# One attention kernel's opening: the first pair of heads projected from all of x and its tokens chosen by 0/1 products

## The chip, the core and the metric

The kernel runs on one core of a Trainium2 chip. A core has a matrix engine (PE, with its weight loads PEld), a vector engine (DVE, VectorE), a scalar engine (ACT, ScalarE), a general engine (POOL, GpSimd) and a sync engine (SP) that here only issues DMAs. Each engine runs its instructions in order; engines wait for each other by semaphores. The metric is the device time of one execution in microseconds (us); three executions give a median.

## The reference

x is (8, 512, 1024): batch, features, tokens; the mask is (8, 1024) of zeros and ones. Cut to what matters:

```python
xt = transpose(x, (0, 2, 1))
q = xt @ Wq.T                                   # queries = keys = values
qh = q.reshape(B, T, 8, 64).transpose(0, 2, 1, 3)
scores = einsum('bhqd,bhkd->bhqk', qh, qh) / 8
logits = (scores * cmask + (1 - cmask) * -1e30) * rmask
attn = softmax(logits)
out = (einsum('bhqk,bhkd->bhqd', attn, qh) -> (B, T, 512)) @ Wo.T
return x + transpose(out, (0, 2, 1))
```

Columns of masked tokens get no weight. Rows of masked tokens have all logits zero, so their context is the plain mean of all values.

## The kernel before, in words

Only kept tokens (mask 1) go through the attention. A batch's kept tokens are compacted into NK columns (NK = 544 here, LONG = 576 is the other size); the last column, NK - 1, carries the batch's mean token, which serves all masked ones. A path for the case that neither size suffices works on all tokens.

**Stages.** `early()` runs once, ahead of a branch; `late(n)` is the attention for n columns. Between them the count of kept tokens (`verdict`) is loaded into a register of every engine, and a branch picks `late(LONG)`, `late(SHORT)` or neither; in program order `late(LONG)` stands first and `late(SHORT)`, which runs here, behind it. At the end a flag is loaded, and a second branch guards the path for all tokens.

**Opening.** `early()` loads the mask and batch 0 of x (`load_batch`, L379: 8 pieces of 256 KB), builds an identity and small constants on POOL, turns the mask into columns (`mcol`), counts ranks of kept tokens by products with a triangle (`rank_t`, L1069 to L1070) and counts per batch (`kept_t`). Batch 0 is turned to rows of tokens by 32 PE transposes (`turn_first`, L406), copied by ACT (L412) and stored in DRAM (`xd`, L416). VectorE sums the rows of x for the mean (`mean_first`, L421) and finds, for each of the NK places, the token that belongs there (`search`, L488: it counts ranks not above the place, over 1024, 896, 768, 640 and 512 columns). Behind the branch, POOL loads Wq (L990), ACT puts its columns in order (`order_columns`, L999), POOL gathers the rows of the kept tokens (`gather`, L500: five indirect DMAs), PE turns them back (`collect`, L513) between the turning of Wq (`turn_weights`, L1009), and the first pair is projected (`project`, L544).

**Pairs.** The attention runs over 32 pairs of heads (8 batches, four pairs each; `pairs[p]`). A pair has five chunks of keys in the order LAST, 0, 1, 2, 3: the chunk LAST is the 64 columns from 512 on (`s` L648, `el` L651), the others have 128 (`s` L626, exponentials `e` L634 with their row sums). Between the chunks, `slots_of(p)` places other work: the contexts of the pair before (`attend_short`, `attend_half`, L672), the projection of the pair after next, its turned values (`turn_values`, `copy_values`), squared lengths and the bound for the softmax (`lengths_of` L592, `bias_of` L605 to L610), and, in the third pair of a batch, the mean and the collecting of the next batch (`put_mean`, `collect`). Dictionaries keyed by (pair, slot) place the turning of later batches by VectorE (`TURN`, L432, stored by SP in four DMAs per quarter, L440), the sums of features by ACT (`FEATURES`, L451), `SEARCH`, `GATHER`, the loads (`LOAD`) and the output's fetches. Names with `_LATER` hold for batch 0 alone. The whole order is written out by hand.

**Buffers.** x has two tiles of half a batch (`x`, bufs = NN = 2), so a batch is loaded into what the batch before leaves. PSUM has two score tiles of two banks (`s`) and four single banks (`t`).

Of the kernel before, what the change touches and what calls it, by code (L numbers as in the profile page):

```python
# [10 lines left out]
F32 = mybir.dt.float32  # L11
# [295 lines left out]
def attention_of_kept_tokens(ctx, tc, x, mask, wq, wo, out, ident, wqT, woT, verdict, flag):  # L307
# [52 lines left out]
    homes = [keep.tile([B * NT, P], F32, name=f"home_{i}") for i in range(2)]  # L360
    seen = {}
# [38 lines left out]

    def turn_first(i):

        r, at = divmod(i * P, NB)
        pt = bank(f"xt_0_{i}")
        for d in range(ND):
            nc.tensor.transpose(pt[:, d * P : (d + 1) * P], xs[0][r][:, d, at : at + P], ident)  # L406
        if i == 0:
            xds[0] = dr.tile([T + 1, D], F32, tag="xd_0", name="xd_0", bufs=1)
            nc.sync.dma_start(xds[0][T : T + 1, :], zero)
        tag = "oc" if i < NC else "xin"  # L410
        xt = sb.tile([P, D], F32, tag=tag, name=f"xt_0_{i}", bufs=NC)
        nc.scalar.copy(  # L412
            xt.rearrange("p (a d f) -> p a d f", a=A, d=ND),
            pt.rearrange("p (d a f) -> p a d f", d=ND, a=A),
        )
        nc.sync.dma_start(xds[0][i * P : (i + 1) * P, :], xt)  # L416

    def mean_first():
        xbars[0] = keep.tile([P, ND, NN], F32, name="xbar_0")
        for r in range(NN):  # L420
            nc.vector.tensor_reduce(xbars[0][:, :, r], xs[0][r], axis=AX.X, op=ALU.add)  # L421
# [43 lines left out]
    def place_ranks(b):  # L465
        rank = sb.tile([P, T], F32, tag="rank", name=f"rank_{b}", bufs=1)
        found = sb.tile([P, NC], F32, tag="found", name=f"found_{b}")
        if b:
            source = sb.tile([P, NC], I32, tag="source", name=f"source_{b}")
        else:  # L470
            source = keep.tile([P, NC], I32, name="source_0")
        searches[b] = rank, found, source
# [35 lines left out]
    def collect(b, i):  # L508
# [8 lines left out]
        nc.scalar.copy(  # L517
            xcs[b][:, :, i * P : i * P + m],
            pt[:, : ND * n].rearrange("p (d n) -> p d n", d=ND)[:, :, :m],
        )  # L520

# [79 lines left out]
    def bias_of(pair):  # L601
# [7 lines left out]
        biases[pair] = sb.tile([P, NC], F32, tag="bias", name=f"bias_{b}_{pr}")  # L609
# [325 lines left out]
    def slots_of(p):  # L935

        b, pr = pairs[p]
# [8 lines left out]
        if p == 0:  # L946
            todo[0].append(lambda: project(behind, 1))
            todo[1].append(lambda: values(behind))
        if behind:
            if p == 0:  # L950
                todo[2].append(lambda: lengths_of(behind))
            elif p != ND - 1:
                todo[1].insert(0, lambda: lengths_of(behind))
        late = p == 2
        if pr == 2 and b + 1 < B:
            at = (2, 2, 2, 3, 3) if late else (1, 2, 2, 2, 2)
            todo[at[0]].append(lambda: put_mean(b + 1))
            for i in range(NC):
                todo[at[i]].append(lambda i=i: collect(b + 1, i))
        if p == ND - 1:  # L960
            todo[3].append(lambda: values(behind))
            todo[3].append(lambda: lengths_of(behind))
        if ahead:
            for hf in range(2):
                todo[4 if late else 3].append(lambda hf=hf: project(ahead, hf))
        if ahead and not late:
# [27 lines left out]
    def order_columns(w, nm):  # L994

        ws = []
        for e in range(ND):
            t = sb.tile([P, D], F32, tag="g", name=f"{nm}_in_order_{e}", bufs=NT)
            nc.scalar.copy(  # L999
                t.rearrange("p (a d f) -> p a d f", a=A, d=ND),  # L1000
                w[e].rearrange("p (a f d) -> p a d f", a=A, d=ND),
            )
            ws.append(t)
        return ws

    def turn_weights(wT, nm, d):
# [5 lines left out]
        nc.scalar.copy(wT[:, d, :], pt)  # L1012

    def early():
# [3 lines left out]
        load_batch(0)  # L1018
# [27 lines left out]
        )  # L1046
        for ri in ris:
            nc.gpsimd.memset(ri, 1.0)

# [13 lines left out]
        nc.vector.tensor_copy(spread, totals.unsqueeze(2).to_broadcast([BC, 2, P]))  # L1063
        pt = bank("mcol_t")
        nc.tensor.transpose(pt[:, :BC], mrow, ident[:BC, :BC])
        mcol = keep.tile([P, BC], F32, name="mcol")
# [8 lines left out]
        nc.tensor.matmul(pk[:, B : B + 1], spread[:, 1, :], ones[:BC, 0:1], start=True, stop=True)  # L1075
        rank = keep.tile([BC, P], F32, name="rank_row")
# [3 lines left out]

        tc.mark_branch_hint_location("over", "LikelyTaken", engines=ENGINES)
        place_ranks(0)
        for r in range(NN):
            pt = bank(f"rank_{r}")
            for i in range(G):
                chunk = r * G + i
                nc.tensor.matmul(
                    pt[:, i * P : (i + 1) * P],
                    ident[:BC, chunk : chunk + 1].to_broadcast([BC, P]),
                    rank,  # L1090
                    start=True,
                    stop=True,
                )
            nc.scalar.copy(searches[0][0][:, r * NB : (r + 1) * NB], pt)  # L1094
            if r == 0:
                for i in range(NT):
                    turn_first(i)

        nc.vector.tensor_scalar(key[DK:P, LAST:NC], key[DK:P, LAST:NC], float(-DK), None, ALU.add)
# [6 lines left out]

        nc.vector.memset(low, 1.0)
        nc.vector.memset(lowest, 1.0)
        nc.vector.memset(flag, 1)
        for b in range(B):  # L1110
            nc.vector.tensor_scalar(pads[:, b, :], key, kept[:, b : b + 1], None, ALU.is_ge)
# [290 lines left out]
```

## Time and profile before

| what | value |
|---|---|
| median of 3 runs | 689.88 us (689.59 to 691.09) |
| the profiled execution's own time | 689.0 us |
| its span, first to last instruction | 687.3 us |
| PE busy | 645.6 us, 94% |
| ACT / DVE / POOL busy | 397.2 / 359.4 / 182.5 us |
| mean granted PE clock | 0.974 |
| DMA | 116.37 MB, 169 GB/s |
| first scores (s, L648) start | 40.06 us |
| second, third, fourth, fifth pair's first scores | 58.11, 72.97, 91.82, 108.71 us |

The busy time by slices of the span (40 slices of 17.2 us each; digits are tenths, 9 is 90% or more):

```profile
PE   6489999999999999999999999999999999999953
PEld 5456566656565655556565655555565656554422
DVE  5235676335464654747464654836564434724462
ACT  4566668755584657655584656665675556454400
POOL 3540310130044202450144202450144102334040
PEclk9799999999999999999999999999999999999985
```

PE is dense from the fourth slice on and thin in the first three; PEclk is the clock that PE was granted. The most costly groups of PE are the scores, contexts, projections and the output product:

```profile
L626 PE MATMUL s<-qT 64*128 64x272 f32 x1024 | 170.1, 417 | 2.9 <-ACT el L651 1.0
L672 PE MATMUL av<-e,v 128*64 128x272 f32 x1024 | 131.4, 399 | 0.0
L544 PE MATMUL pq<-xc,wqT 128*128 128x272 f32 x512 | 124.8, 397 | 0.0
L793 PE MATMUL po<-woT,cT 128*128 128x512 f32 (+1 forms) x448 | 107.5, 434 | 0.0
```

The columns of such a group: line, engine, operation, output from input, shapes, count, then busy us and the mean ns of one, then idle time just ahead and what ended it. A float32 product appears as two records, a transpose as one. Matmul ends are modelled, so the mean of one includes its latency; the pitch of a row of them is the time of the stretch by their number.

### The profile page before, as it was taken

How to read it: one execution, taken by the hardware profiler on the slowest of the kernel's cores; microseconds unless marked ns; L12 is line 12 of the kernel's file. 1: busy time of each engine (PE TensorE's matmuls, PEld its weight loads, DVE VectorE, ACT ScalarE, POOL GpSimd, SP SyncE). 2: the span in 40 equal slices, each digit the busy share in tenths (PEclk: the TensorE clock that was granted, in tenths of full speed). 3: DMA queues.
4: the chain of work that ended last, by engine and by line, in shares of the span. 5: the costliest groups of instructions: out<-in, count | busy, mean ns of one | idle time of the engine just before them, and what ended most of it. 6: DMA issues, size and time to landing. Idle time of an engine off the chain costs nothing.

```text
span 687.3 us, 12044 instructions
## 1 busy us (share of the span) xinstructions
PE 645.6 (94%) x4139; PEld 391.5 (57%) x4139; DVE 359.4 (52%) x1049; ACT 397.2 (58%) x1059; POOL 182.5 (27%) x306
## 2 busy tenths in 40 slices
PE   6489999999999999999999999999999999999953
PEld 5456566656565655556565655555565656554422
DVE  5235676335464654747464654836564434724462
ACT  4566668755584657655584656665675556454400
POOL 3540310130044202450144202450144102334040
PEclk9799999999999999999999999999999999999985
DMA  6473832451766568854876477865764473339358
GB/s 230 155 240 90 253 89 68 141 158 45 169 182 212 155 171 209 269 181 115 210 191 207 156 182 193 261 193 137 190 195 127 114 184 100 113 119 251 84 174 260
DMA packets 96969, 116.37 MB, mean 169 GB/s; under 512 B 10312, under 2 KB 74312, under 8 KB 96896
## 3 DMA queue, kind: packets, MB, share of 16 engines
q1 hardware_dynamic: 80144, 75.13, 40.4%
q0 software_dynamic: 12528, 38.25, 17.4%
q10 hardware_dynamic: 4224, 2.10, 1.0%
q8 instruction: 35, 0.57, 0.3%
q14 instruction: 38, 0.31, 0.1%
HBM read 72.78 MB, written 42.67 MB: 168 GB/s over the span
## 4 chain that ended last, share of the span: by engine, by line
PE 84%; DMA 6%; ACT 3%; DVE 2%; issue 2%; SPq 1%; POOL 1%; POOLq 0%; ACTq 0%; DVEq 0%
PE s L626 21%; PE av L672 19%; PE pq L544 16%; PE po L793 14%; PE s L648 3%; PE xc L513 3%; PE v L569 2%; PE pa L821 2%; PE top L605 1%; ACT e L634 1%; DMA xr<-in_x_dram 1%; DMA xd<-xt 1%; DMA row<-rt 1%; DMA g<-od,origin 1%; PE xt L406 1%
## 5 line engine op out<-in xcount | busy, mean ns | idle before, releaser
L634 ACT ACTIVATE e<-s,bias 128x544 f32<-128x544 f32 x256 | 180.4, 710 | 69.4 <-PE s L626 63.2
L626 PE MATMUL s<-qT 64*128 64x272 f32 x1024 | 170.1, 417 | 2.9 <-ACT el L651 1.0
L626 PEld LDWEIGHTS s<-qT 64*128 64x128 f32 x1024 | 97.7, 186 | 70.6 <-issue 28.9
L672 PE MATMUL av<-e,v 128*64 128x272 f32 x1024 | 131.4, 399 | 0.0
L544 PE MATMUL pq<-xc,wqT 128*128 128x272 f32 x512 | 124.8, 397 | 0.0
L544 PEld LDWEIGHTS pq<-xc,wqT 128*128 128x128 f32 x512 | 97.4, 195 | 18.6 <-issue 0.8
L793 PE MATMUL po<-woT,cT 128*128 128x512 f32 (+1 forms) x448 | 107.5, 434 | 0.0
L672 PEld LDWEIGHTS av<-e,v 128*64 128x64 f32 x1024 | 67.9, 136 | 56.0 <-issue 23.1
L805 POOL DMA_DIRECT2D od<-oc x56 | 30.2, 551 | 251.3 <-ACT oc L803 251.1
L793 PEld LDWEIGHTS po<-woT,cT 128*128 128x128 f32 (+1 forms) x448 | 46.9, 150 | 46.9 <-issue 46.1
L907 POOL DMA_INDIRECT g<-od,block_origin x56 | 57.0, 1017 | 27.1 <-issue 12.4
L867 DVE STREAM_TRANSPOSE o<-g 128x512 f32<-128x512 f32 x56 | 39.3, 702 | 42.6 <-DMA g<-od,block_origin 42.6
L651 ACT ACTIVATE el<-s,bias 128x544 f32<-128x544 f32 x32 | 22.8, 714 | 59.8 <-PE s L648 44.9
L663 DVE CUSTOM_DVE_ANT_0 junk<-el,part 128x272 f32<-128x272 f32 x64 | 28.3, 442 | 53.4 <-ACT el L651 41.2
L592 DVE TENSOR_REDUCE len<-sq 128x10 f32<-128x640 f32 x32 | 26.2, 818 | 52.3 <-ACT sq L590 52.3
L552 ACT COPY qT<-pq 128x272 f32<-128x272 f32 x64 | 24.4, 381 | 49.9 <-PE pq L544 48.3
L903 POOL COPY step<-e 1x1 f32<-1x1 f32 x77 | 15.9, 206 | 136.2 <-ACT e L634 105.7
L634 ACT ACTIVATION_READ_ACCUMULATOR e<-s,bias 128x1 f32 x256 | 50.3, 197 | 0.0
L500 POOL DMA_INDIRECT xin<-xd,source x40 | 39.5, 987 | 20.3 <-issue 6.9
L870 DVE TENSOR_TENSOR xr<-o,xr 128x512 f32<-128x512 f32 x56 | 38.8, 693 | 9.9 <-DMA xr<-in_x_dram 6.9
L607 DVE TENSOR_REDUCE m<-top 128x1 f32<-128x128 f32 x32 | 9.3, 291 | 63.4 <-PE top L605 63.4
L488 DVE TENSOR_SCALAR_CACHE_REDUCE junk<-rank,key 128x1024 f32<-128x1024 f32 (+4 forms) x40 | 40.0, 999 | 3.4 <-ACT rank L1094 2.4
(147 smaller groups left out, 671.0 us busy)
## 6 DMA issues: line engine op xcount, KB each, us to landing
x<-in_x_dram SPq DMA_DIRECT2D x56, 256.0 KB
xd<-xt SPq DMA_DIRECT2D x112, 128.0 KB
xr<-in_x_dram SPq DMA_DIRECT2D x28, 512.0 KB
out_dram<-xr SPq DMA_DIRECT2D x24, 512.0 KB
rb<-row SPq DMA_DIRECT2D x60, 160.0 KB
od<-oc POOLq DMA_DIRECT2D x28, 256.0 KB
rank<-ranks SPq DMA_DIRECT2D x6, 512.0 KB
xd<-xt SPq DMA_DIRECT2D x8, 256.0 KB
```

The costliest lines, as they stand in the source:

```text
L488: nc.vector.tensor_scalar(junk[:, :n], rank[:, i * P :], key[:, col], 0.0, ALU.is_le, ALU.add, accum_out=found[:, col])
L500: nc.gpsimd.indirect_dma_start(out=xin[:n, :], out_offset=None, in_=xds[b], in_offset=bass.IndirectOffsetOnAxis(ap=searches[b][2][:n, i : ...
L544: nc.tensor.matmul(pq[:, :KH], wqT[:, d, pr * P : (pr + 1) * P], xcs[b][:, d, cols], start=(d == 0), stop=(d == ND - 1),)
L626: nc.tensor.matmul(ss[h][:, hf, :KH], qT[heads[h], keys], qT[heads[h], queries[hf]], start=True, stop=True,)
L634: nc.scalar.activation(e[:, :, h, :], ss[h][:, :, :KH], AF.Exp, bias=bias, scale=SCALE, accum_out=sums[pair[1] % 2][:, h, c : c + 1],)
L663: nc.vector.tensor_tensor_reduce(junk[:, :KH], e[:, 0, h, :], parts[b], 1.0, 0.0, ALU.mult, ALU.add, ends[pr % 2][:, h : h + 1])
L672: nc.tensor.matmul(av[head, :KH], v[keys, c, head], e[keys, hf if c < LAST else 0, h, :], start=(c == first), stop=(c == last),)
L793: nc.tensor.matmul(po[k * n : (k + 1) * n, :w], cTs[b, pr][:, i * P : i * P + n], woT[:, pr, k * w : (k + 1) * w], start=(pr == 0), stop=( ...
L805: nc.gpsimd.dma_start(ods[b][places[i], k * w : (k + 1) * w], oc[k * n : (k + 1) * n, :w])
L867: nc.vector.transpose(o.rearrange("p k t -> p (k t)"), gs[b, i])
L870: nc.vector.tensor_tensor(to, o, to, ALU.add)
L907: nc.gpsimd.indirect_dma_start(out=g, out_offset=None, in_=ods[b], in_offset=bass.IndirectOffsetOnAxis(ap=block_origin[:, b, i : i + 1], a ...
```

## The change

Batch 0's first pair no longer waits for the compacted tokens. `early()` now loads the first rows of Wq (into woT's space) and x, and `project_first` projects **all** 1024 tokens onto the first pair's 128 features (`tall`), copies that (`q`), and multiplies it with 0/1 matrices (`chosen`, made by VectorE: `place == count`), which yields the compacted queries (`short`). The bound of that pair comes from the squared lengths of all tokens times the mask. Its tokens' places are found by ACT with Sign and a sum (`search_first`) and turned into sources by one operation. x is turned by VectorE (32x32 blocks, `turn_first`) in place of PE, and stored by SP and POOL. Idle transposes (`warm`) stand around the mask's transpose. Wq's turning, batch 0's mean, collecting and the projections for the second and third pair move into the first pair's slots, with VectorE making the copies. Batch 1's loads move from POOL to SP, and the tables for batch 0 shift. The branch keeps `late(SHORT)` directly behind `early()`; `late(LONG)` goes into the last branch, with an opening of its own.

```diff
+    def load_first():
+        xs[0] = [None] * NN
+        for r in reversed(range(NN)):
...
+                nc.sync.dma_start(
+                    xs[0][r][:, d, :],
+                    x[0].rearrange("(p d) t -> d p t", d=ND)[d][..., r * NB : (r + 1) * NB],
+                )
     def turn_first(i):
-        pt = bank(f"xt_0_{i}")
...
+        xt = sb.tile([P, n // Q, P], F32, tag="xt", name=f"xt_0_{i}", bufs=2)
+        nc.vector.transpose(
+            xt.rearrange("p k (d f) -> p k d f", d=ND),
+            xs[0][r][:, :, at : at + n].rearrange("p d (k t) -> p k d t", t=Q),
+        )
+        for a in range(A):
+            to = xds[0][i * n : (i + 1) * n, a * P : (a + 1) * P]
+            queue = nc.gpsimd if a % 2 else nc.sync
+            queue.dma_start(to.rearrange("(k t) c -> t k c", t=Q), xt[a * Q : (a + 1) * Q, :, :])
+    def add_first(r):
...
+        nc.vector.tensor_reduce(xbars[0][:, :, r], xs[0][r], axis=AX.X, op=ALU.add)
+    def warm(n):
+        pt = bank("warm")
+        for i in range(n):
+            nc.tensor.transpose(pt[:, :P], ident, ident)
+    def choose(i, S):
+        nc.vector.tensor_scalar(S, count[:, : S.shape[1]], place[:, i : i + 1], None, ALU.is_equal)
+    def search_first(rank):
...
+            nc.scalar.activation(
+                sign[:, i * P :], pr[:, i * P :], AF.Sign,
+                bias=half[:, i : i + 1], scale=-1.0, accum_out=found[:, i : i + 1],
+            )
+    def project_first(chosen, mcol):
+        wT = sb.tile([P, ND, P], F32, tag="junka", name="wqT_0", bufs=1)
+        pw = bank("wq_0_t")
+        for d in range(ND):
+            nc.tensor.transpose(pw[:, d * P : (d + 1) * P], woT[:, 0, d::ND], ident)
+        nc.scalar.copy(wT.rearrange("p d e -> p (d e)"), pw)
+        search_first(seen["rank"])
...
+        for i in reversed(range(NT)):
+            project_all(i)
+            if i % 2 == 0:
+                copy_two(i)
+            if i % G == 0:
+                square(i // G)
+        order_columns()
+        turn_first(2)
+        turn_first(3)
+        for i in (3, 2, 1, 0):
+            choose(i, chosen[i])
+        sources_of_first()
+        turn_first(0)
+        turn_first(1)
...
+        lengths(1)
+        lengths(0)
...
+        for i in reversed(range(NT)):
...
+                    nc.tensor.matmul(
+                        short[:, hf, :n],
+                        q[i // G][:, i % G, :],
+                        chosen[i][:, hf * H : hf * H + n],
+                        start=(i == NT - 1),
+                        stop=(i * P <= hf * H),
+                    )
+            if i == G:
+                tops[pairs[0]] = first_top
+                bias_of(pairs[0], first_bias)
+        add_first(1)
+        add_first(0)
+        mean_of(0)
+        nc.scalar.copy(
+            rings[0][:, :LONG].rearrange("p (h n) -> p h n", h=2), short[:, :, :H]
+        )
...
     def slots_of(p):
-        if p == 0:
-            todo[0].append(lambda: project(behind, 1))
-            todo[1].append(lambda: values(behind))
...
-            at = (2, 2, 2, 3, 3) if late else (1, 2, 2, 2, 2)
+            at = (3, 3, 4, 4, 4) if late else (1, 2, 2, 2, 2)
...
+        if p == 0:
+            for d in range(ND):
+                todo[d // 2].append(lambda d=d: turn_weights(wqT, "wq", d, nc.vector.tensor_copy))
+            todo[2].append(lambda: put_mean(0))
+            for i in range(NC):
+                todo[(2, 2, 3, 3, 3)[i]].append(lambda i=i: collect(0, i, nc.vector.tensor_copy))
+            for hf in range(2):
+                todo[3].append(lambda hf=hf: project(behind, hf))
+            todo[4].append(lambda: values(behind))
+            todo[4].append(lambda: lengths_of(behind))
+            for hf in range(2):
+                todo[4].append(lambda hf=hf: project(ahead, hf))
+            todo[4].append(project_first_mean)
+            todo[4].append(lambda: values(pair))
+            todo[4].append(lambda: bias_of(behind))
+        elif p == 1:
+            todo[0].insert(0, lambda: values(behind))
+        elif p == ND - 1:
+            for hf in range(2):
+                todo[1 + hf].append(lambda hf=hf: project(behind, hf))
...
     def late(n):
-        weights["wq"] = order_columns(load_weights(wq, "wq", nc.gpsimd), "wq")
+        queries_of(0)
+        load_batch(1)
...
         for i in range(NC):
             gather(0, i)
...
+        nc.vector.tensor_copy(
+            qT[:, NK:W].rearrange("p (r k) -> p r k", k=END),
+            qT[:, NK - END : NK].unsqueeze(1).to_broadcast([P, (W - NK) // END, END]),
+        )
...
-        TURN_LATER = [(0, 2), (0, 4), (1, 0), (1, 1)]
+        TURN_LATER = [(0, 4), (1, 0), (1, 1), (1, 2)]
+        FEATURES_LATER = {(1, 1): (0,), (1, 2): (1,), (1, 3): (2,), (1, 4): (3,), (2, 0): (4, 5), (2, 1): (6, 7)}
-        GATHER_LATER = {(1, 4): (0, 1, 2), (2, 0): (3,), (2, 1): (4,)}
+        GATHER_LATER = {(1, 4): (0,), (2, 0): (1,), (2, 1): (2,), (2, 2): (3,), (2, 3): (4,)}
...
-        with tc.If(fit > SHORT - 1, label="over") as over:
-            with tc.If(fit < LONG):
...
+    kept_tokens(SHORT)
+    again = nc.values_load(flag[0:1, 0:1], min_val=0, max_val=1)
+    with tc.If(again > 0, label="again"):
+        kept_tokens(LONG)
...
```

More of the change, by code (lines that the diff above doesn't have):

```diff
@@ L935, in slots_of @@
     def slots_of(p):
-        b, pr = pairs[p]
+        b, pr = pair = pairs[p]
         todo = [[] for _ in range(NC)]
@@ L1079, in early @@
         seen["mrow"], seen["rank"] = mrow, rank
[L1081 to L1099, printed above, removed]
+        nc.vector.tensor_tensor(place, pc[:, :NT], mcol[:, :NT], ALU.mult)
+        nc.vector.tensor_scalar(place, place, -1.0, None, ALU.add)
         nc.vector.tensor_copy(kept, pk[:, 0:B])
@@ L1109, in early @@
         nc.vector.memset(flag, 1)
-        for b in range(B):
-            nc.vector.tensor_scalar(pads[:, b, :], key, kept[:, b : b + 1], None, ALU.is_ge)
-        nc.vector.tensor_scalar(pens, pads, NEG, None, ALU.mult)
-        mean_first()
-        for i in range(NC):
-            search(0, i)
-        mean_of(0)
     def place_all():
@@ L1202, in late @@
                 scores(pair, c)
-                if k == (4 if p == ND - 1 else 3) and p + 1 < len(pairs):
+                if k == (4 if p == ND - 1 else 3) and 0 < p < len(pairs) - 1:
                     bias_of(pairs[p + 1])
```

232 lines of the change are left out of this document (160 added, 72 removed).

## The prediction

> **What bounds the kernel now.** I read the busy time by stretches first, then the chain of waits of the first 110 us, then the timeline of the opening, and last the opening in steps of 1 us for the clock. The stretches (columns: PE, PEld, DVE, ACT, POOL busy with counts, granted clock, DMA share, GB/s):
>
> ```profile
> 130.00:210.00 80.00, 79.73 (x527) 48.06 (x524) 39.57 (x121) 51.07 (x141) 19.78 (x33) 1.00 0.55 154
> ...
> 450.00:530.00 80.00, 79.56 (x552) 47.28 (x550) 44.08 (x125) 48.69 (x133) 24.00 (x39) 1.00 0.62 171
> ```
>
> From 130 us to 610 us PE is busy 79.6 of every 80 us. Nothing can be won there by overlap, and a shift of its start is a shift of the end. So the opening decides. The chain there:
>
> ```profile
> 14.98 7.01 DMA xd<-xt
> ...
> 22.90 3.43 DMA xin<-xd,source
> ...
> 40.13 0.62 PE s L648 x8
> ...
> 58.11 0.69 PE s L648 x8
> ...
> 108.71 0.62 PE s L648 x8
> ```
>
> The s L648 rows shown open the first pair of heads, the second, and the fifth, which is batch 1's first (batch 0 has four). Ahead of 40.13 batch 0 goes out to DRAM (7.01 us), comes back by row gather (3.43 us), is turned (PE xc L513 from 26.46), and is projected (pq L544 from 32.31). From the fifth pair on, both kernels issue the same instructions in the same order on each engine, so the change is worth what it moves 108.71. The timeline of the opening:
>
> ```profile
> 8.48 2.29 DVE L421 TENSOR_REDUCE xbar<-x 128x4 f32<-128x2048 f32 x1
> ...
> 11.33 2.29 DVE L421 TENSOR_REDUCE xbar<-x 128x4 f32<-128x2048 f32 x1 [0.56 <-DMA x<-in_x_dram]
> ...
> 21.75 0.17 DVE L458 TENSOR_TENSOR mean<-total,quadrant 128x16 f32<-128x16 f32 x1
> ...
> 25.65 0.17 DVE L1139 TENSOR_SCALAR lacks<-kept 128x8 f32<-128x8 f32 x1 [3.72 <-issue]
> ```
>
> x's row sums cost 4.58 us, hidden now under the turning of x. The branch on the number of kept tokens costs VectorE 3.72 us. The clock, by single microseconds:
>
> ```profile
> 29.00:30.00 1.00, 1.00 (x7) 1.00 (x6) 0.00 (x0) 0.61 (x2) 0.94 (x1) 0.50 0.51 193
> 30.00:31.00 1.00, 1.00 (x10) 1.00 (x9) 0.00 (x0) 0.85 (x2) 0.04 (x1) 0.92 0.04 12
> ...
> 51.00:52.00 1.00, 1.00 (x4) 0.77 (x3) 0.93 (x4) 0.97 (x4) 0.00 (x0) 0.50 0.00 0
> ...
> 54.00:55.00 1.00, 1.00 (x5) 0.80 (x5) 0.00 (x0) 0.39 (x1) 0.00 (x0) 0.97 0.92 170
> ```
>
> PE comes to full clock about 3.6 us after it turns dense (26.46 to 30.1, 50.4 to 54.0) and drops after some 4.7 us of idling (15.3 to 20). Four 128x128 transposes took 0.85 us at half clock, 0.44 at full. The records say 1.00 for the first 19 us, but there too the transposes took 0.85 a group until about 13 us: PE began at half clock.
>
> **The change, part 1: up to the first scores.** Removed from in front of them: the turning of x by PE (32 transposes), its round trip, the turning of Wq, the collecting, the first projection. Added, in PE's order:
>
> Seven and six idle transposes (about 0.21 us each at half clock) fill PE from 1.48, when the identity stands, around mcol_t; rank_t, kept_t and the new place_t (four short records, by kept_t about 0.8) run to about 7.2. The turn of Wq's first rows (0.85) ends at 8.0; those rows are one 256 KB piece put ahead of x, which moves x by about 1 us (1 MB took about 4): its last half, awaited at 11.33 in L421, to 12.3, its first, in use at 8.1, to 9 at the latest. Then 16 rank records (3.4, at half clock), to 11.5.
>
> The tall projection is 64 records of 128 columns: 13.7 us at half clock, 7.0 at full, by the transposes' pitch. The short products: 16 records of 288 columns before the bound (pq: 3.88 us for 16 of 272, so 4.1), then 2.3 us.
>
> If the clock comes up only in the tall products, after one dense stretch like those above, say at 16.4: 23 records are slow, tall ends at 20.9, the first short products at 25.0. If it comes up by 8 to 9, rank ends at 9.5, tall at 16.5 (x's last half is there in time), short at 20.6.
>
> Behind that everything is VectorE in order: the top's transpose and three small steps (1.1, from top L605 to bias L610), the two row sums, now behind the bound (4.6, by L421), mean and constants (0.5), the branch, lacks and the 96 end columns (0.4). The branch now falls through instead of jumping. No row shows that, so between 0 and 3.72; I take 2.0, the middle, for the jump is the only kin. First scores: 25.0 + 8.6 = 33.6 in the late case. In the early case VectorE itself is later than PE (last half of x turned, pads and lengths to about 22.1), and they come at 22.1 + 8.4 = 30.5. The rank products of 6 to 8 us did not raise the clock before 13, which speaks for late, the longer dense stretch for early: 32.5. This moves the opening by 40.1 - 32.5 = 7.6 us.
>
> [...]
>
> Beside this path: eight choosing operations (576 wide, 0.45 to 0.75 us each by 64x128 TENSOR_SCALAR, 0.22, and the 640 wide search, 0.87) and four STREAM_TRANSPOSE of 1.23 fit before 19 us, while PE is in the tall products; without that cover they cost up to 8. With two xt tiles the third turning waits until the first one's stores have landed, and behind it stand pads, lengths and the bound; VectorE waits for the sign counts until about 16.5 anyway, so some 3 us of it are covered. The five sign counts replace VectorE's searches: 3456 columns at ACT's 0.70 per 544, 4.5 us, under the tall products. order_columns (4.07) lies under the short ones. The stores of x are 16 issues instead of 8, half of them on POOL, ahead of its branch, the two part masks (2.0) and the gathers, which start near 24 and land near 32; PE asks for them 5.5 us after the first scores, so 6 us of cover. On SP, batch 1's loads come behind those stores and wait for the row sums to free x's tiles, 28 to 31; they are turned only at the end of the first pair.
>
> **Part 2: from the first scores to 108.71.** Before, 68.6 us. PE's work in it, by the chain's rows at full clock: scores 4 x 5.2, contexts 3 x 4.44, nine half projections of 1.94, values 5 x 0.55, collecting 2.2, Wo 1.74, bounds 1.1, together 59.4; 9.2 us are waits and slow clock, 5.7 of them in the first pair (18.0 us long, with 12.4 of PE work). The change puts into that pair what it took out of the opening: Wq's 16 transposes 1.74, collecting 2.2, half a projection 1.94, values 0.55, the mean's column 0.15, so 6.6 more: 66.0. Of the 9.2 us that were lost, some go, for the first pair now holds 18.4 us of PE work. What remains: PE idles about 5 us before the first scores and starts them slow (1.7), score buffers wait for ACT (about 1.2), copies between projections and values (0.6), and 4 us in the other three pairs, as before, with one new wait: the last gather of batch 1 is asked for one chunk before its transposes, where it had two to three, about 1.3 us. I take 7.5: 73.5. VectorE's nine copies out of PSUM (0.69 each by the 128x512 sum of L845, no less than the 0.44 of the 272 wide L710) lie under the pair's 18 us.
>
> Sum: 32.5 + 73.5 = 106.0 against 108.71: 2.7 us sooner. Against the profiled span of 687.3, 684.6; with the 1.7 around it 686.3. That execution (689.0) lay 0.9 below the median of the three runs, so 687.2.
>
> [...]
>
> **The rivals.**
> - Early: clock full by 9 us, branch nearly free. For it: 7 us of dense PE before the tall products. Against: 6 to 13 us before. First scores at 30.5 or, with the branch at 0.5, near its lower bound, 29: 2 to 3.5 more, 683.7 to 685.2.
> - A wash: the opening's 7.6 us come back as deferred work. For it: 6.6 us of it are PE's, and PE is the bound; with the waits as large as before (9.2 us) the part is 75.2, first scores at 33.5 then end at 108.7: 690.
> - Slower, by the clock: it does not rise until after the first scores are due. Place: tall and short products. Price: 6.7 us for tall, about 4.1 for the first short ones; first scores at 42, 115.5, 696.7. It decides from where the rise comes later than about 20 us, each later microsecond costing a half. For it: full PE from 6.1 to 9.6 without a rise. Against: the two rises 3.6 us after dense starts.
> - Slower, by the new order: gathers of batch 1, the projection moved behind them, VectorE's copies. Price 2 to 4 us over the waits taken: 689 to 692.
>
> **How the numbers follow.** Forecast 0.42 (its own range 685.5 to 689.0), early 0.20, wash 0.14, clock 0.11, order 0.13. A difference under 0.2% (1.4 us) can't be told from none here. Faster: 0.36 + 0.20 + 0.03 = 0.59; same: 0.05 + 0.08 + 0.03 = 0.16; slower: 0.01 + 0.03 + 0.11 + 0.10 = 0.25. Range 683 to 692: it leaves out the slow clock's far end and the best of early.
>
> **What would show it.** First scores at 32 to 33, four pairs in 73 to 74 us, the fifth near 106; transposes and tall records falling from 0.21 to 0.11 us between 8 and 17; the row sums directly ahead of VectorE's branch, and less than 3.7 us for that. Wrong it is if the tall products run slow throughout, if the first pair waits for the gathers, or if a wait of several us stands in pairs two to four.

## The result, and the profile after

| | kernel before | changed kernel |
|---|---|---|
| median | 689.81 us (689.59 to 691.09) | 700.45 us (698.98 to 702.51, 4 runs) |
| ratio | | 1.0153, 95% interval 1.0124 to 1.0182 |
| profiled span | 687.3 us | 699.0 us |
| first scores | 40.06 us | 35.64 us |
| fifth pair's first scores | 108.71 us | 116.18 us |
| from there to the end | 578.6 us | 582.8 us |

The forecast was 687.2 us, with first scores at 32.5 and the fifth pair at 106.0. The changed kernel is 1.5% slower. The first scores do come sooner, by 4.4 us; 11.9 us are lost between them and the fifth pair, and 4.2 more behind it, where both kernels issue the same instructions. From its page, PE, the granted clock, and SP's DMA queue (packets, MB, share of the time of 16 engines):

```profile
PE   8799979999999999999999999999999999999953
...
PEclk7999989999999999999999999999999999999975
...
q1 hardware_dynamic: 82894, 77.23, 42.9%
```

The sixth slice, which was 9, is now 7, and the clock is 8 there: PE waited near 90 us, and ran slowly behind that. The queue's share was 40.4% before, for 75.13 MB. By stretches, the two of the prediction (PE, PEld, DVE, ACT, POOL busy with counts, clock, DMA share, GB/s):

```profile
130.00:210.00 80.00, 79.61 (x533) 47.81 (x533) 36.62 (x119) 51.47 (x140) 16.35 (x28) 1.00 0.50 138
450.00:530.00 80.00, 78.82 (x512) 47.66 (x511) 46.41 (x131) 49.40 (x136) 23.62 (x39) 1.00 0.70 187
```

The early stretch is as dense as before. The late one has lost 0.74 us to waits, and its DMA share went from 0.62 to 0.70. The chain of waits shows the first, fourth and fifth pair open (s L807), and one transfer on the path that was not there:

```profile
35.64 0.91 PE s L807 x8
...
86.51 6.84 DMA xin<-xd,source
...
93.49 0.60 PE xc L659 x4
94.09 1.11 PE s L807 x8
...
116.18 0.62 PE s L807 x8
```

The last gather of batch 1 took 6.84 us from issue to landing, and PE stood in front of it. PE's waits from 36 to 116 us (total, times, longest; the 4.5 us are those that end at the first scores):

```profile
PE s L807 <- DVE qT L1322: 4.5, 1, 4.5
PE xc L659 <- DMA xin<-xd,source: 3.7, 1, 3.7
PE av L831 <- ACT v L736: 1.3, 1, 1.3
PE xc L659 <- DVE cT L936: 1.0, 1, 1.0
```

The three waits of over 1.3 us were each followed by a stretch of half clock, the last from within the wait on (same columns as the stretches above; the clock is the third value from the end):

```profile
36.00:39.40 3.40, 3.40 (x20) 2.41 (x14) 1.60 (x3) 0.81 (x2) 0.00 (x0) 0.50 0.97 354
...
76.90:80.30 3.40, 3.40 (x16) 1.60 (x16) 1.79 (x10) 3.35 (x9) 1.35 (x2) 0.51 0.79 224
...
90.60:97.40 6.80, 3.91 (x26) 2.42 (x28) 4.43 (x22) 1.07 (x3) 0.35 (x1) 0.50 0.42 129
```

In the kernel before only one such stretch of 3.4 us lies between the first scores and the fifth pair, from 50.6 us on. The opening, PE's timeline (start, length, idle time before and what ended it):

```profile
10.38 3.78 PE L493 MATMUL tall<-wqT,x 128*128 128x128 f32 x16
15.95 3.45 PE L493 MATMUL tall<-wqT,x 128*128 128x128 f32 x16 [1.79 <-ACT q L503]
20.36 2.05 PE L493 MATMUL tall<-wqT,x 128*128 128x128 f32 x16 [0.96 <-ACT sq L510]
22.88 2.05 PE L493 MATMUL tall<-wqT,x 128*128 128x128 f32 x16 [0.46 <-ACT q L503]
...
28.76 2.39 PE L555 MATMUL short<-chosen,q 128*128 128x288 f32 x12
35.64 0.91 PE L807 MATMUL s<-qT 64*64 64x272 f32 x8 [4.50 <-DVE qT L1322]
```

The long projection stood still three times, 3.2 us in all, for ScalarE's copies and squares of its own results, and its first half ran at half clock. Full clock had come once before, for a single stretch, and went again at 8.7 us though PE's records leave no gap before that (columns as above):

```profile
5.30:8.70 3.40, 3.40 (x25) 2.95 (x24) 1.48 (x9) 0.84 (x2) 0.75 (x2) 1.00 1.03 316
8.70:18.90 10.20, 8.41 (x39) 7.89 (x38) 7.43 (x15) 5.22 (x11) 3.72 (x7) 0.50 0.76 253
```

Behind the last short product PE idles 4.50 us. VectorE's timeline there:

```profile
29.61 4.47 DVE L435 TENSOR_REDUCE xbar<-x 128x4 f32<-128x2048 f32 x2
...
35.16 0.18 DVE L1311 TENSOR_SCALAR lacks<-kept 128x8 f32<-128x8 f32 x1 [0.58 <-issue]
```

The row sums stand where the prediction had them, and the branch that falls through costs 0.58 us where the jump cost 3.72. Behind the fifth pair, PE's waits from 116 to 620 us have a row that the kernel before does not have:

```profile
PE top L764 <- DVE top L758: 4.3, 4, 1.4
```

The chain leads from there to a gather of finished rows (start, us, what):

```profile
278.77 10.38 DMA g<-od,block_origin
...
289.18 0.72 DVE o L1026
...
293.57 0.17 DVE top L758
...
293.79 0.32 PE top L764
```

VectorE takes its work in order: the squared lengths and their maximum (`top`) stand behind `o` and `xr` of the rows that came late (`o` and `xr` are VectorE's two steps on finished rows: it turns them and adds the residual). Measured from one first pair of a batch to the next, batches 1 to 6 take 76.3, 76.4, 76.5, 76.5, 76.5, 76.4 us before, and 76.3, 76.3, 77.7, 77.4, 77.0, 77.2 after.

### The profile page after: what moved, and what is told of

Its sections match the earlier page's. It is cut to its first block, busy times and chain, and to the rows that moved or that the text cites. A ratio compares the mean times of both kernels' runs of the same rounds, so it can differ in the third digit from the quotient of the medians.

```text
span 699.0 us, 12228 instructions
## 1 busy us (share of the span) xinstructions
PE 657.0 (94%) x4212; PEld 400.1 (57%) x4212; DVE 366.5 (52%) x1061; ACT 395.0 (57%) x1055; POOL 181.6 (26%) x304
## 3 DMA queue, kind: packets, MB, share of 16 engines
q1 hardware_dynamic: 82894, 77.23, 42.9%
## 4 chain that ended last, share of the span: by engine, by line
PE 77%; DMA 9%; DVE 4%; issue 2%; ACT 1%; SPq 1%; POOL 0%; POOLq 0%; DVEq 0%; ACTq 0%
PE s L785 19%; PE av L831 17%; PE po L952 14%; PE pq L703 14%; DMA g<-od,block_origin 3%; PE xc L659 3%; PE s L807 3%; PE v L728 2%; PE pa L980 2%; DMA xr<-in_x_dram 1%; PE top L764 1%; DVE xr L1029 1%; DMA xin<-xd,source 1%; DMA xd<-xt 1%; DMA g<-od,origin 1%
## 5 line engine op out<-in xcount | busy, mean ns | idle before, releaser
L793 ACT ACTIVATE e<-s,bias 128x544 f32<-128x544 f32 x248 | 174.7, 709 | 68.0 <-PE s L785 65.8
L785 PE MATMUL s<-qT 64*128 64x272 f32 x1024 | 168.4, 418 | 1.0 <-issue 0.7
L831 PE MATMUL av<-e,v 128*64 128x272 f32 x1024 | 133.1, 403 | 0.0
L703 PE MATMUL pq<-xc,wqT 128*128 128x272 f32 x496 | 119.3, 393 | 0.0
L703 PEld LDWEIGHTS pq<-xc,wqT 128*128 128x128 f32 x496 | 93.1, 193 | 17.8 <-issue 0.8
L1066 POOL DMA_INDIRECT g<-od,block_origin x56 | 56.4, 1007 | 50.2 <-DVE o L1026 12.4
L711 ACT COPY qT<-pq 128x272 f32<-128x272 f32 (+1 forms) x62 | 23.6, 381 | 51.7 <-PE pq L703 49.1
L793 ACT ACTIVATION_READ_ACCUMULATOR e<-s,bias 128x1 f32 x248 | 48.6, 196 | 0.0
L1029 DVE TENSOR_TENSOR xr<-o,xr 128x512 f32<-128x512 f32 x56 | 38.8, 693 | 14.5 <-DMA xr<-in_x_dram 8.0
L581 DVE STREAM_TRANSPOSE xt<-x 128x1024 f32<-128x1024 f32 x28 | 34.8, 1242 | 3.2 <-DMA xd<-xt 3.1
```

What stands on the lines that cost most here:

```text
L581: nc.vector.transpose(xt.rearrange("p k (d f) -> p k d f", d=ND), xs[b][r][:, :, at : at + n].rearrange("p d (k t) -> p k d t", t=Q),)
L703: nc.tensor.matmul(pq[:, :KH], wqT[:, d, pr * P : (pr + 1) * P], xcs[b][:, d, cols], start=(d == 0), stop=(d == ND - 1),)
L785: nc.tensor.matmul(ss[h][:, hf, :KH], qT[heads[h], keys], qT[heads[h], queries[hf]], start=True, stop=True,)
L793: nc.scalar.activation(e[:, :, h, :], ss[h][:, :, :KH], AF.Exp, bias=bias, scale=SCALE, accum_out=sums[pair[1] % 2][:, h, c : c + 1],)
L831: nc.tensor.matmul(av[head, :KH], v[keys, c, head], e[keys, hf if c < LAST else 0, h, :], start=(c == first), stop=(c == last),)
L1029: nc.vector.tensor_tensor(to, o, to, ALU.add)
```

## What the experiments tell apart

Three questions: why the same instructions run slower behind the fifth pair; what the lost time of the second to fourth pair is; what the opening could have given. Each of three groups of runs has its own chip and runs the kernel before beside the others (median 685.6, 685.3 and 689.8 us; chips differ), so the ratios to it are compared, and within a trace the stretches.

### Where xr lies

The program gives every buffer an address. The buffer for the residual, xr, lay at 184064 before, a multiple of 256, and lies at 49856 after, 192 bytes over one, since the change uses it early for `chosen` and so has it laid out earlier. All 1 KB packets of SP's queue between 270 and 560 us are loads into xr and stores from it. By the trace's packet records they take 67.9 ns in the kernel before, 79.4 in the changed one; 512-byte packets take 29.2 in both. Two kernels move xr, one moves the scratch tensors in DRAM.

In a_xr, the changed kernel:

```diff
+        sb.tile([P, 16], F32, tag="gap", name="gap", bufs=1)
         room = sb.tile([P, D // Q, T // A], F32, tag="xr", name="chosen", bufs=1)
+        sb.tile([P, 48], F32, tag="gap2", name="gap2", bufs=1)
```

> The changed kernel, its buffer xr (residual blocks of x, 1 KB rows) moved by 64 bytes per partition: it starts at a multiple of 256 bytes, as in the kernel before (184064), where the change has put it at 49856 (192 over such a multiple); a second gap of 192 bytes behind it leaves every later buffer at its old offset modulo 256. In the changed kernel's trace the 1 KB packets on the SP queue take 79 ns each between 270 and 560 us, before 68, while 512-byte packets take 29.2 in both; batches 3 to 6 take 77.69, 77.39, 76.99 and 77.23 us from first pair to first pair where before they take 76.4 to 76.5. Theory A (the place of xr in SBUF makes its transfers longer, and they push the gathers of the outputs back until bias_of waits): 1 KB packets back to 67 to 70 ns, those batches back to 76.3 to 76.5, 4 us less in all, about 696.5. Theory B (the scratch tensors' place in DRAM): packets stay at 79, batches stay, 700.4. Theory C (the phase that batch 0's delays leave the queues in): the same as B.

In b_xr, the kernel before:

```diff
+            sb.tile([P, 48], F32, tag="gap", name=f"gap_{b}", bufs=1)
             xrs[b] = sb.tile([P, D // Q, T // A], F32, tag="xr", name=f"xr_{b}", bufs=1)
```

> The kernel before, with 192 bytes put ahead of xr alone (and of o, which no transfer touches), so that xr starts 192 bytes over a multiple of 256, as in the changed kernel. Theory A: 1 KB packets go from 68 to about 79 ns between 270 and 560 us, batches 3 to 6 grow from 76.4 by up to 1.2 us each, the time by 1 to 4 us, 691 to 694. Theories B and C: 68 ns, 76.4 us and 689.8 us as before.

In a_dram:

```diff
+    away = dr.tile([11910, D], F32, name="away", bufs=1)
     ranks = dr.tile([B * NT, P], F32, name="ranks", bufs=1)
...
+        nc.gpsimd.dma_start(away[0:1, :], zero)
         xds[0] = dr.tile([T + 1, D], F32, tag="xd_0", name="xd_0", bufs=1)
```

> The changed kernel with an unused 24.4 MB tensor in front of its scratch tensors in DRAM, of which one row is written once, so that the copies of x, the outputs by kept token and the rows of inverses lie at the addresses that they have in the kernel before (xd_1 at 26607616 and not 2215936). Theory B: batches 3 to 6 at 76.4, 1 KB packets near 68 ns, 4 us less, about 696.5. Theories A and C: unchanged, 77.3 us a batch, 79 ns, 700.4.

| | xr over 256 B | 1 KB packet, 270 to 560 us | batches 1 to 6, us |
|---|---|---|---|
| a_xr | 0 | 70.1 ns | 76.0, 75.9, 75.9, 75.9, 75.9, 75.9 |
| b_xr | 192 | 77.6 ns | 76.0, 76.0, 76.9, 76.8, 76.1, 76.1 |
| a_dram | 192 | 78.0 ns | 76.0, 75.9, 78.2, 76.2, 77.4, 75.9 |

The line of the profile's page for SP's queue shows it too. For the kernel before, a_xr and b_xr, in this order:

```profile
q1 hardware_dynamic: 80144, 75.13, 40.4%
```

```profile
q1 hardware_dynamic: 82894, 77.23, 40.4%
```

```profile
q1 hardware_dynamic: 80144, 75.13, 42.6%
```

Between the first and the third, packets and MB are equal, and the share of time is not; a_xr has the changed kernel's packets and MB, with 40.4% where that has 42.9. For packets and batches theory A holds in both directions, and B falls: with the scratch tensors at their old addresses packets stay at 78.0 ns, and batches 3 and 5 stay long. The time of b_xr is 690.06 against 685.57 us, a ratio of 1.0072 (1.0040 to 1.0103): 192 bytes of shift alone make the kernel before slower, by a little more than expected. But the time did not follow in the changed kernel: a_xr's ratio was 1.0153 (1.0101 to 1.0206), no better than the changed kernel's, and a_dram's 1.0135 (1.0084 to 1.0187). a_xr's first scores had come at 40.40 us, in a_dram at 39.45, in the changed kernel at 35.64, with the same opening. So the changed kernel and a_xr's (as a_xr2) were run side by side, with one more offset:

> The changed kernel itself, beside the three below on one chip, since chips differ (the kernel before took 689.9 us where the changed kernel was timed, 685.6 and 685.3 where the seven edits were). By its first measurement: a ratio of 1.0153 to the kernel before; batches 3 to 6 longer than 76.0 us, 1 KB packets at 78 to 79 ns. If the opening's luck (when the clock first rises) made up the first ratio, 1.011 to 1.020.

> The kernel of a_xr again, beside the changed kernel itself. Theory A (the place of xr lengthens batches 3 to 6): every batch at 75.9, and the ratio to the kernel before 0.003 to 0.006 below a_again's. If it is not below it by 0.002, the longer packets are real but the time that they cost is not in what is timed.

> The kernel before with xr 128 bytes over a multiple of 256 (184192), beside 0 in the kernel before (68 ns for a 1 KB packet between 270 and 560 us) and 192 in b_xr (77.6). If a packet is cut where it crosses 256 bytes at any offset: 76 to 79 ns. If only 64-byte offsets hurt (192 is 64 over a multiple of 128): 67 to 70 ns.

a_again: 702.22 us, ratio 1.0181 (1.0148 to 1.0214). a_xr2: 699.68, 1.0126 (1.0097 to 1.0156). That is 2.5 us by the medians, 3.8 by the ratios; the intervals overlap by 0.0008. Batches 3 to 6 took 76.2, 76.6, 76.6, 77.2 in a_again and 76.2, 76.3, 77.0, 76.2 in a_xr2, whose packets took 71.5 ns: of a_again's loss of 1.8 us, measured by batches 1 and 2, 0.8 is left, in one batch. By time the gain is thus barely clear of noise; by the traces it is clear. Against four times the mean of batches 1 and 2, batches 3 to 6 lose 1.3 to 4.3 us in the eight traces with xr at 192 (1 KB packets at 76.3 to 79.4 ns), and at most 0.8 in the six others (67.9 to 71.9 ns). What sets the amount between 1.3 and 4.3 is not shown; theory C, the phase in which batch 0 leaves the queues, may have a part in it. In b_xr128 a packet took 71.9 ns, batches 76.3 to 76.6, and its only run 691.16 us: the harm is in 192, little if any in 128, and the 67 to 70 ns expected for the second case is just missed. Against the 67.9 ns of the kernel before, a packet took 1.06 at 128, and 1.14 (77.6 ns) and 1.17 (79.4 ns) at 192; from a multiple of 256 the changed kernel's variants took up to 71.5 ns, 1.05. Why 192 costs that much is not shown: that a packet is cut at such multiples was an assumption of the first case, whose 76 to 79 ns did not come at 128.

### The transfers of batch 1 and 2

In the changed kernel SP issues eight loads for batch 2 in one go, ahead of the last gather of batch 1, since the row of inverses in front of them holds up SP (2.2 us of waiting for it between 77 and 84 us); VectorE's third turn waits for a store:

```profile
83.46 4.38 SPq L385 DMA_DIRECT2D x<-in_x_dram  x8
```

```profile
68.04 1.25 DVE L581 STREAM_TRANSPOSE xt<-x 128x1024 f32<-128x1024 f32 x1 [3.05 <-DMA xd<-xt]
```

First the loads alone (a_load):

```diff
-        LOAD_LATER = {(2, 1): (0, 1), (2, 2): (2, 3), (2, 3): (4, 5), (2, 4): (6, 7)}
+        LOAD_LATER = {(1, 4): (0, 1, 2, 3), (2, 4): (4, 5), (3, 0): (6, 7)}
```

> The changed kernel with the eight loads of x for batch 2 asked for at other steps: four at the last step of the second pair, two at the last of the third and two at the first of the fourth, where it asks for two at each of the last four steps of the third pair; there SP, which waits for the row of inverses before them, issued all eight from 83.46 to 87.84 us, around the last gather of batch 1 (asked for at 86.51, awaited by PE until 93.49, after an idle 3.73). Theory 1 (that gather shares the engines with 2 MB of loads): it lands within 3 us, the 3.73 us wait and the half clock from 94.0 to 97.4 go (1.7 us), the fifth pair starts 3 to 5.5 us sooner than 116.1, and the time falls by as much, about 695 to 697.5. Theory 2 (an indirect transfer takes 6 to 7 us anyway when it is the last of five, or is held up by the rows and stores): the wait stays over 2.5 us, the fifth pair starts at 115 to 116, and the time is within 1.5 us of 700.4.

The wait for the gather went, as theory 1 has it (by the packet records its rows landed 2.7 us after the issue at 85.94, where the changed kernel's took 6.2), and another came. PE's waits, and VectorE's timeline:

```profile
PE top L764 <- DVE top L758: 3.0, 1, 3.0
```

```profile
85.02 1.28 DVE L634 TENSOR_SCALAR_CACHE_REDUCE junk<-rank,key 128x1024 f32<-128x1024 f32 x1 [4.95 <-DMA rank<-ranks]
```

The first four loads now stand ahead of batch 2's ranks on SP. The ranks came late, and behind the search that waits for them stands the bound of the next pair. From first scores to fifth pair it took 77.5 us, 3.0 less than the changed kernel; but five traces with the old order (the changed kernel's two, a_xr, a_xr2, a_dram) took 77.8 to 80.5, and the time, 697.69 us, ratio 1.0170 (1.0118 to 1.0222), shows no gain. Then all that was in the wrong order (a_turn):

```diff
-        TURN_LATER = [(0, 4), (1, 0), (1, 1), (1, 2)]
+        TURN_LATER = [(0, 4), (0, 4), (1, 0), (1, 2)]
-        FEATURES_LATER = {(1, 1): (0,), (1, 2): (1,), (1, 3): (2,), (1, 4): (3,), (2, 0): (4, 5), (2, 1): (6, 7)}
+        FEATURES_LATER = {(1, 1): (0,), (1, 2): (1,), (1, 3): (2, 3), (2, 0): (4, 5), (2, 1): (6, 7)}
-        LOAD_LATER = {(2, 1): (0, 1), (2, 2): (2, 3), (2, 3): (4, 5), (2, 4): (6, 7)}
+        LOAD_LATER = {(2, 4): (4, 5), (3, 0): (6, 7)}
-        GATHER_LATER = {(1, 4): (0,), (2, 0): (1,), (2, 1): (2,), (2, 2): (3,), (2, 3): (4,)}
+        GATHER_LATER = {(1, 4): (0, 1, 2), (2, 0): (3,), (2, 1): (4,)}
...
                         load_ranks(b + 2)
+                        for i in () if b else range(ND):
+                            load_piece(b + 2, i)
```

> The changed kernel with the second turn of batch 1 one step earlier (behind the first), the third and fourth one step earlier and at the same step, four of batch 2's loads right behind its ranks, the rest after the last gather, batch 1's gathers at the steps that they have in the kernel before, and one of ScalarE's sums of features a step earlier. Theory 1 (batch 0's later pairs lose to transfers that are asked for in the wrong order): VectorE's wait of 3.05 us for the stores of xt, PE's of 3.73 us for the last gather and VectorE's of 2.38 us for the ranks all go; PE's idle time between the first scores and the fifth pair falls from 6.1 to under 2.5 us, the half clock behind it (10.2 us at half in the trace of the changed kernel after 70 us) to 3.4 or none; that stretch takes 74 to 76 us in place of 80.5, and the time falls by 4 to 6 us, 694.5 to 696.5. Theory 2 (the queues are simply full there): other waits take their place, the stretch takes 78 us or more, and the time 698 or more.

By pairs from first scores to fifth pair, the first and the third of the four:

```profile
37.89:60.13 22.24, 22.24 (x136) 16.55 (x136) 10.55 (x22) 10.25 (x30) 0.00 (x0) 0.90 0.48 159
...
75.38:89.14 13.76, 13.76 (x110) 8.63 (x110) 8.40 (x33) 12.56 (x35) 6.01 (x10) 1.00 0.75 247
...
```

The clock is full from the second pair on, and PE waits nowhere for more than 0.15 us. The stretch takes 72.7 us for 80.5; the third pair alone went from 21.4 to 13.8. The time is 691.13 us, ratio 1.0073 (1.0048 to 1.0098), 8 to 11 thousandths under the changed kernel's two ratios. Theory 1 holds; how the gain divides among the edits is not shown.

### The opening

a_sums moves the row sums into VectorE's idle time:

```diff
         lengths(1)
+        add_first(1)
+        add_first(0)
+        mean_of(0)
         lengths(0)
...
-        add_first(1)
-        add_first(0)
-        mean_of(0)
```

> The changed kernel with VectorE's two row sums over x (xbar, 4.47 us together) and the mean issued between the two reductions of squared lengths, where VectorE idles 4.84 us, and no longer behind the bias, where they hold up the branch. Theory 1 (they, and the branch behind them, are what stands between the last short product and the first scores): PE's idle time before the first scores falls from 4.50 us to about 1 us (ScalarE's copy of qT, 0.64, and the edge copy), the time by 3 to 4 us, 696.5 to 697.5 where the kernel before has 689.9. Theory 2 (the branch or the gathers hold the first scores anyway): idle stays at 4 us or more and the time within 1 us of 700.4. How late the first scores start in all is no test, since the clock's first rise has come anywhere from 5 to 28 us in five traces.

PE's timeline:

```profile
29.84 2.39 PE L558 MATMUL short<-chosen,q 128*128 128x288 f32 x12
33.34 0.69 PE L807 MATMUL s<-qT 64*64 64x272 f32 x8 [1.11 <-DVE qT L1322]
```

The idle time fell from 4.50 to 1.11, as theory 1 has it. The time is 695.05 us, ratio 1.0134 (1.0112 to 1.0156), 2 to 5 thousandths better; the intervals overlap, so by time alone the gain is not shown. a_tall gives the long projection a PSUM bank for every two chunks:

```diff
-        tall = ps.tile([P, 2, NB], F32, tag="s", name="tall")
+        tall = {}
...
+            if i % 2:
+                tall[i // 2] = bank(f"tall_{i // 2}")
...
-                    tall[:, r, at : at + P],
+                    tall[i // 2][:, i % 2 * P : (i % 2 + 1) * P],
...
-            nc.scalar.activation(sq[:, at], tall[:, r, :], AF.Square)
+            nc.scalar.activation(sq[:, at], q[r].rearrange("p c e -> p (c e)"), AF.Square)
```

> The changed kernel with the long projection of the first pair in four tiles of one PSUM bank each, not in one tile of two banks, and the squares taken from the copies. Theory 1 (PE's three waits in it, 1.79, 0.96 and 0.46 us behind ScalarE's copies and squares, come from sharing one tile): all three go, and from the first of these 64 records to the last PE runs through; 2 to 3.2 us less in the opening, about 697.5. Theory 2 (ScalarE itself, with 5 us of signs ahead of the first copy, is the bound): the waits move to the products with the 0/1 matrices (L555), 16 us behind the start at the earliest, and the time stays within 1 us of 700.4.

```profile
10.31 10.04 PE L495 MATMUL tall<-wqT,x 128*128 128x128 f32 x64
20.19 4.05 PE L557 MATMUL short<-chosen,q 128*128 128x288 f32 x16
```

All three waits are gone, and none came in front of the short products; 64 records take 10.04 us where they took 14.5 with the waits. The time is 691.07 us, ratio 1.0075 (1.0052 to 1.0097), 5 to 7 us better than the changed kernel by the ratios, about twice what was expected. Part of that may be the clock: with the waits (eight traces of this opening, the changed kernel's two among them) full clock comes to stay at 16.9 to 27.9 us, without them (a_tall, a_all, a_best) at 15.3 to 16.2.

### All together

> The changed kernel with the three edits of a_sums, a_tall and a_turn and the buffer xr at a multiple of 256 bytes, as in a_xr. If the losses are these four and add up: 3.5 (row sums) + 2.5 (PSUM tile) + 5 (order of batch 1's transfers) + 4.2 (xr) = 15 us off the changed kernel, 685 where the kernel before takes 689.9, a ratio of 0.993. If they cover each other, or the half clock comes back elsewhere: 690 to 694, a ratio of 1.000 to 1.006.

681.49 us against 685.33, ratio 0.9945 (0.9926 to 0.9965): faster than both kernels. By the ratios it is 14 to 16 us better than the changed kernel, where 15 were expected if the four losses add up. The four pairs of batch 0 take 70.6 us, with no wait of PE over 0.15 us and full clock throughout. One wait was new, in the opening, for now the sums delay the lengths:

```profile
26.73 0.29 PE L766 MATMUL top<-ident,first_top 128*128 128x128 f32 x1 [2.71 <-DVE first_top L551]
```

a_best puts one sum between the two reductions of lengths, the other behind the maximum, and gives pads and penalties to GpSimd:

```diff
         lengths(1)
         add_first(1)
-        add_first(0)
-        mean_of(0)
         lengths(0)
...
             first_top, first_len.rearrange("p c h -> p (c h)"), axis=AX.X, op=ALU.max
         )
+        add_first(0)
+        mean_of(0)
...
-            nc.vector.tensor_scalar(pads[:, b, :], key, kept[:, b : b + 1], None, ALU.is_ge)
-        nc.vector.tensor_scalar(pens, pads, NEG, None, ALU.mult)
+            nc.gpsimd.tensor_scalar(pads[:, b, :], key, kept[:, b : b + 1], None, ALU.is_ge)
+        nc.gpsimd.tensor_scalar(pens, pads, NEG, None, ALU.mult)
```

> The kernel of a_all with the first pair's squared lengths served sooner: one row sum between the two reductions, the other with the mean behind the maximum, and the pads and penalties made by GpSimd, which idles from 13.7 to 17.7 us there, so that PE's wait of 2.71 us for first_top in a_all's trace goes. If that wait was on the path: first scores 1.5 to 2.5 us sooner relative to the end of the long projection (10.1 us in a_all, from 20.15 to 30.27), a ratio to the kernel before of 0.991 to 0.993 where a_all has 0.9945. If the branch behind VectorE's work sets the first scores: less than 0.7 us, 0.994.

```profile
12.86 8.97 PE L495 MATMUL tall<-wqT,x 128*128 128x128 f32 x64
21.67 4.05 PE L560 MATMUL short<-chosen,q 128*128 128x288 f32 x16
...
29.25 0.69 PE L809 MATMUL s<-qT 64*64 64x272 f32 x8 [1.20 <-issue]
```

The wait is gone; from the end of the long projection to the first scores it takes 7.4 us (21.83 to 29.25) where a_all took 10.1. The trace shows a loss too, in the first pair:

```profile
34.82 1.88 PE L787 MATMUL s<-qT 64*128 64x272 f32 x8 [1.72 <-ACT e L795]
```

ScalarE's exponentials come late there, for a reason that the trace does not show; half clock follows from 36.6 to 40.1 us, and from first scores to fifth pair it takes 74.5 us where a_all took 70.6. So in these two traces the fifth pair comes later in a_best, at 103.75 against 100.84. The time is 681.93 us against 689.76, ratio 0.9879 (0.9856 to 0.9902), and the six batches take 76.1 to 76.2 us. The medians of a_best and a_all are alike, the ratios are not; they ran on different chips, and whether a_best is better than a_all is open.

## Why the prediction was wrong

The forecast's span was 684.6 us, the profiled one 699.0. By its own steps the 14.4 us are 3.1 in the opening (35.6 for 32.5), 7.0 from first scores to fifth pair (80.5 for 73.5) and 4.2 behind it (582.8 for 578.6). Two of these steps failed in their mechanism, the largest in its size.

**"The same instructions in the same order, so the change is worth what it moves 108.71": this failed, by 4.2 us.** Order and instructions are the same, the addresses are not. A buffer that the change uses earlier was laid out elsewhere, its 1 KB packets took 17% longer, and in batches 3 to 6 gathers came late, VectorE with them, and PE waited. a_xr, a_xr2 and b_xr show in both directions that the place of xr is the cause; that the longer packets are what makes the gathers late is read from the chain alone. 3.4 us of the 4.2 lie in batches 3 to 6, at the upper end of what xr's place cost in any trace (a_again lost 1.8), and of the remaining 0.8 it is not shown how much is xr's.

**The waits of batch 0, taken at 7.5 us: foreseen in kind, wrong in size.** This is the largest miss, 7.0 us. PE's added work of 6.6 us was about right: by a_all's 70.6 us without waits, against 64.9 of PE's busy time before, of which a half-clock stretch of 3.4 us took up to 1.7, it is 5.7 to 7.4. But the prediction counted 9.2 us as lost before, where the trace has 3.7 of waits and up to 1.7 of slow clock: its 59.4 us of PE's work stand against 64.87 us busy (in the first pair 12.4 against 15.79). It let the loss shrink to 7.5. In truth it grew from at most 5.4 to about 9.9 (80.5 - 70.6): 6.1 of waits and the rest slow clock behind them. Of the "one new wait" for batch 1's last gather it had the place; it was 3.73 us, not 1.3, as it priced the distance in chunks and not what SP would send just then. It missed that SP's loads would pile up behind the row of inverses. Of the rival by the new order the mechanism was right; a_turn, with another order, took 7.8 us less in this stretch, about twice the upper end of its price of 2 to 4. That a wait between the pairs costs a second time through the clock was not in the sum; it had a slow start for the first scores alone (1.7).

**The opening: the tail was right, the middle was not.** The row sums stood on the path for 4.47 us (4.6 forecast), the branch took 0.58 (0 to 3.72, 2.0 taken; the early rival's 0.5 was nearer). But the long projection was costed as 64 records in a row: it has three waits of 3.2 us, behind ScalarE, whose five signs come first (3840 columns and 5.0 us, not 3456 and 4.5) and whose copies share a PSUM tile with the products. The clock rose later too, at 18.9 for 16.4 us. And one trace is no measure of this opening: in seven traces of kernels with it unchanged the first scores start between 35.6 and 40.4 us, 37.9 in the mean; the three traces of the old opening have 38.8 to 40.9, mean 39.9. By these means the change gains 2 us there, not 7.6.

**The rivals by the clock.** The late one (first scores at 42) came nearly whole in a_xr: three of the four groups of long products ran at half clock, full clock came at 27.9 us, and the first scores at 40.4. The early one did not come: in four of the eleven traces with warming transposes full clock came at 4.8 to 5.6 us, but for 3.4 us only, and was gone before the long projection.

## What to carry to other kernels

Where a change moves nothing of an instruction stream but lays its buffers out anew, compare the addresses: a buffer of 1 KB rows did best at a multiple of 256 bytes here (67.9 to 71.5 ns a packet there; 192 bytes over one made its packets 12 to 17% longer than the 67.9), and a queue's share of time at equal bytes shows when it lies elsewhere (42.6% for 40.4). Work that is moved to a denser place needs its transfers looked at by queue: what stands in front of them on SP, what is sent beside them, and which engine's order is held up when one is late. Price a wait of PE with the half clock that may follow (here 3.4 us of it behind the wait of 1.34 us, 6.8 us from within that of 3.73), and let the order of small steps on VectorE (here 4.5 us of sums) be set by who waits behind them.

## What the runs showed of the hardware

In the traces of the two kernels the stretches from one change of the granted clock to the next were 3.41, 6.83, 10.24, 17.07, 20.48 and 37.55 us long up to 97.4 us (1, 2, 3, 5, 6 and 11 times 3.413), and in the 14 traces stretches of half clock of 3.4, 6.8, 10.2, 13.7 and 17.1 us occur ahead of the last 35 us. The changes had no fixed place with respect to the start: the first rise came at 4.8 to 27.9 us in 14 traces (13.10 in the kernel before, 5.25 in the changed one). A wait of PE of 2.6 us or more between the pairs came with half clock in each of the eight traces that have one (from within the wait, or up to 1.2 us behind it); the wait of 1.34 us was followed by it in five of eight. In the changed kernel full clock went at 8.7 us with no gap in PE's records from 1.42 us on.
